# Layer 0 of a four-layer convolution mixer: two channels' banded matrices in one 64x64 block instead of one channel's in a 32x32 block, and tile 0 normalised from two tiles of the input

## The chip, the cores and the metric

The kernel runs on one core of a Trainium2 chip. TensorE (PE) multiplies matrices, VectorE (DVE), ScalarE (ACT) and GpSimd (POOL) work on tiles in on-chip memory, SyncE (SP) and ACT issue most of the transfers. The metric is the device time of one execution in microseconds; the median of the runs before the change is 3408.86 us (3407.19 to 3410.58). All data is float32.

## The reference

The input `x` is (8, 384, 32, 32): 8 images, 384 channels. Four layers follow each other, each behind a group normalisation over 12 neighbouring channels. What matters here is layer 0, which begins with three depthwise 3x3 convolutions of the same normalised input:

```python
def _dwproj(x, dw, g, b, pw):
    y = lax.conv_general_dilated(x, dw, (1, 1), ((1, 1), (1, 1)), feature_group_count=C, ...)
    y = jax.nn.gelu(_bn(y, g, b), approximate=False)      # batch norm over images and pixels
    return jnp.einsum('oc,bchw->bohw', pw, y)
q, k, v = (_dwproj(x, dw, g, b, pw) for each of q, k, v)
attn = softmax(q.T k * scale);  out = bn(w_out @ (attn v))
```

Layer 1 is a mixture of four expert networks, layer 2 a depthwise 7x7 convolution, layer 3 a mixture of small MLPs and depthwise convolutions. They are changed only in the place where a helper and a constant are defined.

## The kernel before

The 384 channels lie in three tiles `ct` of 128 partitions. Layer 0 goes in these stages.

**Statistics.** For each of the 8 images two loads bring tile 0 (into `x0`, L258) and tiles 1 and 2 (into `x`, L259). DVE takes `bn_stats` and `bn_aggr` of each tile and image (L144, L263): 24 pairs (tile, image). `gn_coefs` (L146, L264) then makes scale and shift of the group normalisation for all tiles at once: small matmuls over neighbouring tiles for the mean, four DVE operations, the same matmuls for the variance, a power on GpSimd (L139, `gn_s`), one more DVE operation (`gn_t`).

**Preparing a tile.** `prepare0(ct, b)` normalises an image of a tile on ACT (`affine`, L204) and transposes it in 32x32 blocks on DVE into `xt0s[ct]` (L284), so that the image column lies on the partitions: partition 32 i + (column), and the channel is a free index. For tiles 1 and 2 it first loads the image again into `xn` (3 buffers).

**Convolution.** A 3x3 convolution of one channel is then, for each of three rows of taps, a matmul with a banded 32x32 matrix over the columns. There are 36 groups `n` = (tile, which of q/k/v, u of 4), each with 8 x 4 = 32 channels. In a group (L322 to L333) the host's matrices `w` (384 KB, loaded by ACT's queue three groups ahead, 4 buffers) are used as 32x32 blocks: 2 x 3 x 4 x 4 = 96 matmuls of 32x32 against 256 columns, sixteen positions of the array in turn. The profile records two passes for each float32 matmul, so a group is 192 records. The result fills `ps`, four banks of PSUM; there are two such buffers, all of PSUM. ACT copies `ps` into `o` (L354, 128x2048). Four groups fill one `o` (m = n // 4 counts them, 9 in all); there are two buffers of `o`.

**Results.** While the groups of m run, DVE takes the eight images of m - 1 from `o` (`results`, L299): a transpose back into `y` (4 buffers), two `bn_stats`, and SP writes `y` to `raw` in device memory. After the last m the eight images are taken on their own, the batch norm's coefficients follow (`coefs0`, L210 to L214), and attention begins, which needs them and `raw`.

**Order.** In layer 0 the instructions of PE, ACT and DVE stand in the order in which the program names them (`manual_schedule`); those of GpSimd and SP are placed by a scheduler. In the loop over groups a step names, in this order: the matmuls of `n`, the load of the weights of `n + 3`, the preparations (tile 1 in the four groups of m = 0, two images each; tile 2 in m = 3 to 5), the results of m - 1, and ACT's copy of `n`. Each engine works through its queue in order, so that a waiting instruction holds all behind it.

The changed helper `Banks` (L1113) hands out parts of one PSUM buffer to small matmuls in later layers, and `parity` (L1033 to L1036) is a 128x2 constant: column 0 is one on the partitions of even blocks of 32, column 1 on those of odd blocks. Layer 2 uses it to spread two channels' banded matrices into 64x64 blocks (`next_weights`, L1068, both halves on ACT) and multiplies 64x64 by 64x256 (L1332).

Of the kernel before, what the change touches and what calls it, by code (L numbers as in the profile page):

```python
# [38 lines left out]

# [3 lines left out]
ORDER_0 = ORDER_A.reshape(NC, 4, 4, 8).swapaxes(1, 2).ravel()  # L43
# [30 lines left out]

@with_exitstack
def conv_mixer_kernel(ctx: ExitStack, tc: tile.TileContext, a: dict, out: bass.AP):
# [12 lines left out]
    nc.gpsimd.memset(mhalf, -0.5)  # L89

# [152 lines left out]
    with (  # L243
# [9 lines left out]
        with tc.tile_pool(name="cx", bufs=4) as cx, tc.tile_pool(  # L253
            name="cgn", bufs=2, space=PSUM
        ) as cgn:
            for b in range(B):
                x = cx.tile([P, NC - 1, N], FP, tag="x", name="x")
                nc.sync.dma_start(out=x0[:, b], in_=a["x"][b, :, 0])  # L258
                nc.sync.dma_start(out=x, in_=a["x"][b, :, 1:])  # L259
                for ct in range(NC):  # L260
                    bs = xst[:, ct, 2 * b : 2 * b + 2, :]
                    bn_stats_of(bs, x[:, ct - 1, :] if ct else x0[:, b])
                    nc.vector.bn_aggr(mvx[:, :, ct, b], bs.rearrange("p a s -> p (a s)"))  # L263
            s0, t0 = gn_coefs((mvx[:, 0], mvx[:, 1]), cgn)  # L264

        with tc.tile_pool(name="cy", bufs=3, reuse_waits="tile") as cy, tc.tile_pool(
# [4 lines left out]
            def prepare0(ct, b):  # L271

                if b == 0:
                    pool = cxb if ct == 1 else cxa
                    xt0s[ct] = pool.tile([P, 32, B, H + 2], FP, tag="xt0", name="xt0")
                    for row in (0, H + 1):
                        nc.gpsimd.memset(xt0s[ct][:, :, :, row : row + 1], 0.0)
                if ct == 0:
                    xn = x0[:, b]
                else:  # L280
                    xn = cy.tile([P, N], FP, tag="xn", name="xn")
                    nc.sync.dma_start(out=xn, in_=a["x"][b, :, ct, :])
                affine(xn, xn, s0[:, ct, b : b + 1], t0[:, ct, b : b + 1])
                nc.vector.transpose(  # L284
                    xt0s[ct][:, :, b, 1 : 1 + H].rearrange("p c h -> p h c"), img(xn)
                )
# [4 lines left out]
            def weights_of(n):  # L291
                if n < len(groups):
                    w = cy.tile([P, 2, 4, 3, W], FP, tag="w", name="w", bufs=4)
                    nc.scalar.dma_start(out=w, in_=a["w0"][groups[n]])
                    weights0[n] = w

# [16 lines left out]
            for n in range(3):  # L313
                weights_of(n)
            for b in range(B):
                prepare0(0, b)
            last_o, last = None, None
            for n, (ct, v, u) in enumerate(groups):
# [3 lines left out]
                w = weights0.pop(n)  # L322
                ps = cps.tile([P, 4, 2, B, H], FP, tag="ps", name="ps")
                for cc in range(2):
                    for k in range(3):
                        for j in range(4):
                            for i in range(4):
                                r = slice(32 * i, 32 * i + 32)
                                nc.tensor.matmul(  # L329
                                    ps[32 * j : 32 * j + 32, i, cc],  # L330
                                    lhsT=w[r, cc, j, k, :],
                                    rhs=xt0s[ct][r, 8 * j + 2 * u + cc, :, k : k + H],
                                    start=k == 0, stop=k == 2,  # L333
                                )
                weights_of(n + 3)
                m = n // 4
                if m == 0:
                    for b in (2 * u, 2 * u + 1):
                        prepare0(1, b)
# [693 lines left out]
    parity = lw.tile([P, 2], FP, name="parity", bufs=1)  # L1033
    nc.gpsimd.memset(parity, 0.0)
    for i in range(4):
        nc.gpsimd.memset(parity[32 * i : 32 * i + 32, i % 2 : i % 2 + 1], 1.0)  # L1036
# [76 lines left out]
    class Banks:  # L1113
        def __init__(self):
            self.banks, self.used = tp.tile([P, 4, HF], FP, tag="ps", name="ps"), 0

        def tile(self, shape, *_, **__):
            n = int(np.prod(shape[1:]))
            v = self.banks[: shape[0], self.used, :n]
            self.used += 1  # L1120
            if len(shape) == 3:
                v = v.rearrange("p (a b) -> p a b", b=shape[2])
            if len(shape) == 4:
                v = v.rearrange("p (a b c) -> p a b c", b=shape[2], c=shape[3])
            return v
# [194 lines left out]
    with tc.manual_schedule(engines=ORDERED | {mybir.EngineType.Pool}):  # L1320

        for ct in range(NC):
            o = None
            for c in range(8):
# [28 lines left out]
                if ct == 2 and c == 5:  # L1353
                    norm01 = gn_steps((mv3[:, 0, :2], mv3[:, 1, :2]), Banks, order="B")
                    next(norm01)
# [36 lines left out]
        norm3 = gn_steps((mv3[:, 0], mv3[:, 1]), Banks, order="B")  # L1392
# [8 lines left out]
        pb = Banks().tile([MR, B])  # L1401
# [80 lines left out]
        def hidden3(i):  # L1482


            slot, units = Banks(), []
# [37 lines left out]
        def branch_mean():  # L1523

            hs = atile("hs", [B], MR)
            nc.vector.tensor_add(hs, hsum[:, :, 0], hsum[:, :, 1])
            slot = Banks()
            pa = slot.tile([P, 2, B])
            for j in range(2):
                nc.tensor.matmul(  # L1530
                    pa[:, j], lhsT=mw2[:, j * P : (j + 1) * P], rhs=hs, start=True, stop=True
                )
            nc.vector.tensor_add(mean[:, 1:3], mean[:, 1:3], pa)
            for ct in range(NC):
                nc.vector.tensor_scalar(
                    mean[:, ct], mean[:, ct], 1.0 / N, bsum[:, ct : ct + 1], ALU.mult, ALU.add
                )

            pf = slot.tile([96, B])
            for ct in range(NC):  # L1540
                nc.tensor.matmul(
                    pf, lhsT=fw1[:, ct, :], rhs=mean[:, ct], start=ct == 0, stop=ct == NC - 1
                )
            nc.scalar.activation(g1, pf, AF.Gelu, bias=fb1)
# [3 lines left out]
        def branch_weights():  # L1548

            pg = Banks().tile([P, NC, 3, B])  # L1550
# [60 lines left out]
        def output_bias():  # L1611
            po = Banks().tile([P, NC, B])
# [60 lines left out]
        def first():  # L1673
            wms[0] = weights3(0, Banks())
            c0s[0] = begin(0, 0, pre, 2, nc.gpsimd)
# [64 lines left out]
def lay_out(inp):  # L1740
# [12 lines left out]
    def tiles_0(v):  # L1753
        return tiles(v, ORDER_0)

# [14 lines left out]
    band = band.reshape(3, NC, 4, 4, 4, 2, 3, W, W)  # L1770
    o["w0"] = band.transpose(1, 0, 4, 2, 7, 5, 3, 6, 8).reshape(NC, 3, 4, P, 2, 4, 3, W)
    gb = [np.stack([tiles_0(f[f"L0_conv_{k}_{v}"]) for k in "gb"], 2) for v in qkv]
    o["bn_gb"] = np.concatenate(gb, 1)
    o["bn_gbo"] = np.stack([tiles(f[f"L0_conv_{k}_out"]) for k in "gb"], 2)
    for v in "qk":
        pad = np.zeros((C, NP, 2, 64), np.float32)
        pad[..., 1 : 1 + HD] = f[f"L0_conv_pw_{v}"].T.reshape(C, NP, 2, HD)
        o[f"pw_{v}s"] = tiles_0(pad.reshape(C, NP, P))
        w = f[f"L0_conv_pw_{v}"].T.reshape(C, NP, 3, 32)
        w = np.stack([w[:, :NC, 0], w[:, :NC, 1], w[:, NC], w[:, :NC, 2]], 2)  # L1780
        o[f"pw_{v}"] = tiles_0(w.reshape(C, NC, P))
    o["pw_v"] = tiles_0(f["L0_conv_pw_v"].T)
# [100 lines left out]
```

## Time and profile before

| what | value |
|---|---|
| median of three runs | 3408.86 us |
| the profiled execution | 3404.2 us, its span 3402.5 us |
| statistics end, first normalisation begins | 40.1 us, 50.5 us |
| first and last copy of `ps` begin | 71.8 us, 314.4 us |
| first result's transpose begins | 94.0 us |
| last `bn_stats` of the results ends | 337.8 us |
| PE, 6912 records of L329 | 169.2 us busy |
| DVE, busy from 94 to 338 us | 194.5 us |

Times are from the start of the span. A row of a table of groups reads: line, engine, operation, out<-in, shapes, count | busy time, mean ns of one | idle time before it and what ended it. A row of windows gives the busy time of each engine in a stretch with the number of instructions, the granted TensorE clock as a share of full speed, the busy share of the 16 DMA engines and GB/s.

### The profile page before, as it was taken

How to read it: one execution, taken by the hardware profiler on the slowest of the kernel's cores; microseconds unless marked ns; L12 is line 12 of the kernel's file. 1: busy time of each engine (PE TensorE's matmuls, PEld its weight loads, DVE VectorE, ACT ScalarE, POOL GpSimd, SP SyncE). 2: the span in 40 equal slices, each digit the busy share in tenths (PEclk: the TensorE clock that was granted, in tenths of full speed). 3: DMA queues.
4: the chain of work that ended last, by engine and by line, in shares of the span. 5: the costliest groups of instructions: out<-in, count | busy, mean ns of one | idle time of the engine just before them, and what ended most of it. 6: DMA issues, size and time to landing. Idle time of an engine off the chain costs nothing. (4 is left out here: it accounts for less than half of the span.)

```text
span 3402.5 us, 46860 instructions
## 1 busy us (share of the span) xinstructions
PE 3116.7 (92%) x20224; PEld 1427.8 (42%) x20224; DVE 1608.2 (47%) x2193; ACT 1305.0 (38%) x1339; POOL 157.6 (5%) x361
## 2 busy tenths in 40 slices
PE   3666999999999999999997999999999999985989
PEld 2444334343434333333433444444444444665534
DVE  6787344444454544444453365344333332256164
ACT  3655353544444443535333402122122111556530
POOL 1000000000000000000000000000000000111300
PEclk9988999999999999999998999999999999997999
DMA  6665301011101111110006423121221110676766
GB/s 228 241 245 215 122 21 68 30 58 40 58 22 56 42 56 42 40 56 21 21 22 230 138 64 87 55 76 37 63 72 40 51 42 19 220 243 205 242 202 200
DMA packets 96734, 339.47 MB, mean 100 GB/s; under 512 B 14312, under 2 KB 16960, under 8 KB 91144
## 3 DMA queue, kind: packets, MB, share of 16 engines
q1 hardware_dynamic: 72520, 266.95, 23.2%
q10 hardware_dynamic: 13776, 36.90, 3.5%
q0 software_dynamic: 10224, 32.56, 2.8%
q8 instruction: 160, 2.62, 0.3%
q14 instruction: 54, 0.44, 0.0%
HBM read 237.18 MB, written 102.32 MB: 100 GB/s over the span
## 5 line engine op out<-in xcount | busy, mean ns | idle before, releaser
L552 ACT ACTIVATE e<-sc 128x1024 f32<-128x1024 f32 x512 | 484.3, 1030 | 583.9 <-PE sc L545 583.6
L976 PE MATMUL y<-hs,w 128*128 128x512 f32 x1152 | 521.5, 594 | 6.8 <-DVE hs L961 6.7
L763 PE MATMUL ph<-xn,w 128*128 128x512 f32 x1152 | 525.1, 594 | 0.3 <-ACT xn L204 0.3
L545 PE MATMUL sc<-qT,kT 64*128 64x512 f32 x2048 | 481.0, 606 | 22.6 <-DVE qT L471 15.4
L564 PE MATMUL av<-e,vT 128*64 128x512 f32 x2048 | 469.2, 600 | 0.0
L767 ACT ACTIVATE hs<-ph,b 128x512 f32<-128x512 f32 x192 | 131.6, 685 | 637.9 <-PE ph L763 636.2
L976 PEld LDWEIGHTS y<-hs,w 128*128 128x128 f32 x1152 | 217.2, 190 | 282.6 <-issue 258.6
L763 PEld LDWEIGHTS ph<-xn,w 128*128 128x128 f32 x1152 | 216.4, 190 | 268.2 <-issue 259.4
L545 PEld LDWEIGHTS sc<-qT,kT 64*128 64x128 f32 x2048 | 186.3, 186 | 309.6 <-issue 231.7
L961 DVE TENSOR_TENSOR hs<-hs,cb 128x512 f32<-128x512 f32 x192 | 130.0, 687 | 377.2 <-ACT hs L767 371.3
L564 PEld LDWEIGHTS av<-e,vT 128*64 128x64 f32 x2048 | 136.0, 137 | 319.1 <-issue 319.1
L453 PE MATMUL sc<-y,pw 128*128 128x512 f32 x576 | 252.7, 600 | 11.9 <-DVE kT L471 7.1
L329 PE MATMUL ps<-xt,w 32*32 32x256 f32 x6912 | 169.2, 438 | 99.4 <-issue 99.3
L580 DVE RECIPROCAL inv<-sm 128x512 f32<-128x512 f32 x64 | 214.6, 3353 | 2.2
L578 DVE LOAD_MASK_SELECT sm<-av x64 | 0.9, 14 | 417.1 <-PE av L564 417.1
L329 PEld LDWEIGHTS ps<-xt,w 32*32 32x32 f32 x6912 | 115.2, 110 | 153.1 <-issue 129.5
L1332 PE MATMUL ps<-xt,wx 64*64 64x256 f32 x2688 | 160.8, 399 | 20.1 <-ACT wx L1068 14.7
L453 PEld LDWEIGHTS sc<-y,pw 128*128 128x128 f32 x576 | 109.9, 192 | 154.3 <-issue 146.1
L354 ACT COPY o<-ps 128x2048 f32<-128x2048 f32 x36 | 134.6, 3738 | 101.2 <-PE ps L329 100.5
L966 DVE SCALAR_TENSOR_TENSOR r<-cb,b,r 128x512 f32<-128x512 f32 x192 | 134.3, 745 | 69.1 <-DMA cb<-cfmem 67.5
L1068 ACT ACTIVATE wx<-w,parity 128x448 f32<-128x448 f32 (+2 forms) x192 | 108.3, 616 | 103.3 <-PE ps L1332 32.5
L1332 PEld LDWEIGHTS ps<-xt,wx 64*64 64x64 f32 x2688 | 109.2, 140 | 70.5 <-ACT wx L1068 17.0
(292 smaller groups left out, 2771.5 us busy)
## 6 DMA issues: line engine op xcount, KB each, us to landing
raw<-y SPq DMA_DIRECT2D x72, 512.0 KB
y<-raw SPq DMA_DIRECT2D x24, 1536.0 KB
xr<-in_x SPq DMA_DIRECT2D x42, 512.0 KB
cb<-cfmem SPq DMA_DIRECT2D x64, 256.0 KB
w<-in_w ACTq DMA_DIRECT2D x36, 384.0 KB
x<-in_x SPq DMA_DIRECT2D x16, 768.0 KB
z<-z POOLq DMA_DIRECT2D x16, 768.0 KB, 4.2
r<-z SPq DMA_DIRECT2D x24, 512.0 KB
```

Of the source, the lines that this page charges most:

```text
L329: nc.tensor.matmul(ps[32 * j : 32 * j + 32, i, cc], lhsT=w[r, cc, j, k, :], rhs=xt0s[ct][r, 8 * j + 2 * u + cc, :, k : k + H], start=k == ...
L354: nc.scalar.copy(o.rearrange("p b h (i c) -> p i c (b h)", i=4)[:, :, 2 * u : 2 * u + 2], ps.rearrange("p i c b h -> p i c (b h)"),)
L453: nc.tensor.matmul(ps[:, h, :], lhsT=w[:, ct, pair, :], rhs=y[:, ct, h * HF : (h + 1) * HF], start=ct == 0, stop=ct == NC - 1,)
L545: nc.tensor.matmul(sc[:, s, :], lhsT=kTs[b][r, pair, m * P : (m + 1) * P], rhs=qTs[b][r, pair, h * HF : (h + 1) * HF], start=True, stop=True,)
L552: nc.scalar.activation(e, sc, AF.Exp, scale=1.0 if shifted else HD**-0.5)
L564: nc.tensor.matmul(av[64 * s : 64 * s + 64, :], lhsT=vT[:, m, c0 : c0 + 64], rhs=e[:, s, :], start=m == 0, stop=m == N // P - 1,)
L580: nc.vector.reciprocal(inv, sm)
L763: nc.tensor.matmul(ph, lhsT=w1[:, e, ct, dc * P : (dc + 1) * P], rhs=xn[:, ct, :], start=ct == 0, stop=ct == NC - 1,)
L767: nc.scalar.activation(hs, ph, AF.Relu, bias=b1[:, e, dc : dc + 1])
L966: nc.vector.scalar_tensor_tensor(out=out[oc], in0=cb[e], scalar=b2[:, oc, e : e + 1], in1=out[oc], op0=ALU.mult, op1=ALU.add,)
L976: nc.tensor.matmul(py[oc], lhsT=w2[:, e, dc, oc * P : (oc + 1) * P], rhs=hs, start=k == 0, stop=k == len(TODO) - 1,)
L1332: nc.tensor.matmul(ps[64 * d : 64 * d + 64, 2 * i + e, c % 2], lhsT=w[r, d * K7 + k, :], rhs=xts[ct][r, 16 * d + 8 * e + c, :, k : k + H], ...
```

## The change

The host lays the banded matrices so that two channels are stacked in 64 partitions; `w` has the same bytes. For each group, `spread0` writes them into a `wx` of twice the size: ACT writes the left half (times `parity` column 0), GpSimd the right half (times column 1), so that each 64x64 block holds two channels' 32x32 matrices on its diagonal and zeros beside. A group is then 2 x 3 x 8 = 48 matmuls of 64x64 against 256 columns (96 records). The weights have 3 buffers instead of 4, `wx` has 3; at step `n` the spread of `n + 2` and then the load of `n + 3` are named.

At the start only tiles 0 and 1 are loaded and measured (8 images each), and tile 0 is normalised with coefficients made from them: its groups reach no further than tile 1. The eight images of tile 2 are loaded into `xn` and measured at steps 0 and 1, the mean's matmuls stand on PE after group 1 and the variance's after group 2, each in one of the two PSUM buffers, and the preparation of tile 1 moves from steps 0 to 3 to steps 3, 4, 8, 9 and 10.

```diff
+    parity = const.tile([P, 2], FP, name="parity")
+    nc.gpsimd.memset(parity, 0.0)
+    for i in range(4):
+        nc.gpsimd.memset(parity[32 * i : 32 * i + 32, i % 2 : i % 2 + 1], 1.0)
...
+        def x_stats(ct, b, x):
+            bs = xst[:, ct, 2 * b : 2 * b + 2, :]
+            bn_stats_of(bs, x)
+            nc.vector.bn_aggr(mvx[:, :, ct, b], bs.rearrange("p a s -> p (a s)"))
-        with tc.tile_pool(name="cx", bufs=4) as cx, tc.tile_pool(
+        with tc.tile_pool(name="cx", bufs=8) as cx, tc.tile_pool(
...
-                x = cx.tile([P, NC - 1, N], FP, tag="x", name="x")
+                x = cx.tile([P, N], FP, tag="x", name="x")
                 nc.sync.dma_start(out=x0[:, b], in_=a["x"][b, :, 0])
-                nc.sync.dma_start(out=x, in_=a["x"][b, :, 1:])
-                for ct in range(NC):
...
-            s0, t0 = gn_coefs((mvx[:, 0], mvx[:, 1]), cgn)
+                nc.sync.dma_start(out=x, in_=a["x"][b, :, 1])
+                x_stats(0, b, x0[:, b])
+                x_stats(1, b, x)
+            norms = {0: gn_coefs((mvx[:, 0, :2], mvx[:, 1, :2]), cgn)}
...
-                    w = cy.tile([P, 2, 4, 3, W], FP, tag="w", name="w", bufs=4)
+                    w = cy.tile([P, 24, W], FP, tag="w", name="w")
                     nc.scalar.dma_start(out=w, in_=a["w0"][groups[n]])
...
+            def spread0(n):
+                if n < len(groups):
+                    w = weights0[n]
+                    x = weights0[n] = cy.tile([P, 24, 2, W], FP, tag="wx", name="wx")
+                    nc.scalar.activation(x[:, :, 0, :], w, AF.Copy, scale=parity[:, 0:1])
+                    nc.gpsimd.tensor_scalar(x[:, :, 1, :], w, parity[:, 1:2], None, ALU.mult)
+            def slot0():
+                ps = cps.tile([P, 4, 2, B, H], FP, tag="ps", name="ps")
+                return Slot(ps.rearrange("p i c b h -> p i (c b h)"))
+            def stats2(b):
+                xn = cy.tile([P, N], FP, tag="xn", name="xn")
+                nc.sync.dma_start(out=xn, in_=a["x"][b, :, 2, :])
+                x_stats(2, b, xn)
...
-                        for j in range(4):
-                            for i in range(4):
-                                r = slice(32 * i, 32 * i + 32)
-                                nc.tensor.matmul(
-                                    ps[32 * j : 32 * j + 32, i, cc],
-                                    lhsT=w[r, cc, j, k, :],
-                                    rhs=xt0s[ct][r, 8 * j + 2 * u + cc, :, k : k + H],
+                        for e, d, i in product(range(2), repeat=3):
+                            r = slice(64 * i, 64 * i + 64)
+                            nc.tensor.matmul(
+                                ps[64 * d : 64 * d + 64, 2 * i + e, cc],
+                                lhsT=w[r, 12 * cc + 6 * e + 3 * d + k, :],
+                                rhs=xt0s[ct][r, 16 * d + 8 * e + 2 * u + cc, :, k : k + H],
...
+                spread0(n + 2)
                 weights_of(n + 3)
                 m = n // 4
-                if m == 0:
-                    for b in (2 * u, 2 * u + 1):
-                        prepare0(1, b)
+                if n < 2:
+                    for b in range(4 * n, 4 * n + 4):
+                        stats2(b)
+                if n == 1:
+                    norm = gn_steps((mvx[:, 0], mvx[:, 1]), slot0)
+                    next(norm)
+                if n == 2:
+                    norms[1] = norms[2] = next(norm)
+                for b in {3: (0, 1), 4: (2, 3), 8: (4, 5), 9: (6,), 10: (7,)}.get(n, ()):
+                    prepare0(1, b)
```

`Slot` is the old `Banks` with its PSUM buffer given from outside; later layers call it through a function `banks()`. `parity` leaves layer 2. The order of channels in the host's vectors of layer 0 follows the new stacking.

## The prediction

> **What bounds the kernel now.** I read the stages first, by windows, then who waits in layer 0, then the instructions' order in time, and last the rows of layer 2, which holds the new matmul's form. Layer 0 takes the first 340 us of 3402.5; nothing behind it changes, so a microsecond won before attention begins is won for the whole.
>
> The windows (busy time of PE, PEld, DVE, ACT, POOL; clock; DMA share; GB/s) show PE as good as idle for 50 us while the input is measured, and then no engine full: PE 65 to 70%, DVE 65 to 94%.
>
> ```profile
> 0.00:25.00 25.00, 8.27 (x28) 6.71 (x28) 18.26 (x40) 5.16 (x15) 7.12 (x25) 1.00 0.93 368
> 100.00:150.00 50.00, 33.50 (x1516) 22.84 (x1505) 35.75 (x44) 31.37 (x11) 1.06 (x2) 0.97 0.59 214
> 150.00:225.00 75.00, 48.43 (x2008) 32.71 (x1977) 70.26 (x79) 46.67 (x17) 0.00 (x0) 0.90 0.74 259
> 225.00:300.00 75.00, 52.30 (x2060) 35.42 (x2044) 48.67 (x66) 38.92 (x11) 0.85 (x1) 0.85 0.64 225
> ```
>
> The waits of 94 to 338 us say whom they wait for: DVE for ACT's copies, ACT (page's groups: 100.5 us) for the matmuls, and the matmuls for "issue", that is for nothing but their own instructions.
>
> ```profile
> DVE y L299 <- ACT o L354: 35.8, 6, 10.1
> ...
> PE ps L329 <- issue: 72.4, 44, 4.5
> ```
>
> In order of time the matmuls come in packets of 128 records, 2.75 us long (21.5 ns a record), with 0.7 to 4.5 us between packets:
>
> ```profile
> 115.22 2.74 PE L329 MATMUL ps<-xt,w 32*32 32x256 f32 x127 [2.18 <-issue]
> 119.05 2.74 PE L329 MATMUL ps<-xt,w 32*32 32x256 f32 x128 [1.09 <-issue]
> 122.50 2.75 PE L329 MATMUL ps<-xt,w 32*32 32x256 f32 x128 [0.71 <-issue]
> ```
>
> From the first copy to the last (71.8 to 314.4 us) 35 groups take 6.93 us each, 36 ns a record. So the count of PE's instructions bounds layer 0, except in 150 to 225 us, where DVE is 94% busy. Behind PE stand these:
>
> ```profile
> L354 ACT COPY o<-ps 128x2048 f32<-128x2048 f32 x36 | 134.6, 3738 | 101.2 <-PE ps L329 100.5 <-ACT xn L204 0.8
> L144 DVE BATCH_NORM_STATS2 stats<-y 128x6 f32<-128x512 f32 x144 | 92.7, 686 | 2.5
> L299 DVE STREAM_TRANSPOSE y<-o 128x1024 f32<-128x1024 f32 x72 | 88.4, 1228 | 36.0 <-ACT o L354 35.8
> L284 DVE STREAM_TRANSPOSE xt<-xn 128x1024 f32<-128x1024 f32 x16 | 29.9, 1929 | 22.4 <-ACT xn L204 22.4
> L204 ACT ACTIVATE xn<-xn,gn_t,gn_s 128x1024 f32<-128x1024 f32 x16 | 19.2, 1239 | 0.7 <-DMA xn<-in_x 0.7
> ```
>
> **The change, part by part.**
>
> *Start.* DVE measures one tile of one image every 1.39 us (starts at 37.22 and 38.61), so 16 instead of 24 save 11.2 us; the transfers set nearly the same end: 8.4 MB of input, 1.2 of weights and 0.5 of constants at 368 GB/s are 27.3 us. I put the end at 30 instead of 40.1 us. The normalisation's coefficients take 10.4 us now (40.1 to 50.5). The last tile's mean loses 6 of 12 records of 0.237 us (-1.4), the variance 6 of 14 (-1.3), GpSimd's power 16 columns instead of 24 (a 128x16 row later is 2.91 us, this one 4.21: -1.3): 6.4 us. The first normalisation begins at 36.5 instead of 50.5; the eight transposes end 15.3 us later as now, at 51.8. ACT's first two spreads stand ahead of it and wait for weights; the loads stand behind one that goes out at 20.6 us now, so they land in time.
>
> *Then the third tile's statistics.* They are moved with their eight loads, past nothing on SP but behind all 16 loads of the start; three have free buffers. On DVE they stand behind the transposes: 8 x 1.39 us, plus some 1.2 us for buffers, end at 64. Groups 0 and 1 run beside that (5.2 us each, 1.9 more for the first at a cold clock, where layer 2's first 56 records after idle time take 5.5 us instead of 3.0: 58.9 and 64.1). Then PE's queue holds the mean (3.2 us, to 67.3), and behind it group 2, which also waits for the copy of group 1 (67.9): to 73.1. Behind that the variance (76.2), the power (80.7), and ACT's two normalisations, which stand ahead of the copy of group 3 (to 87.3); the next two images' normalisations and transposes end at 92.6, and only then does DVE take the first result. It does so at 94.0 now. So of 14 us only 1.4 are left, and four of tile 1's transposes (7.4 us) are still owed. This part alone would gain nothing; it counts for what it leaves DVE.
>
> *Matmuls.* Layer 2 in its undisturbed stretch runs the new form:
>
> ```profile
> 2910.00:2940.00 30.00, 30.00 (x556) 20.79 (x550) 0.00 (x0) 21.25 (x23) 3.76 (x10) 1.00 0.30 85
> ```
>
> 556 records in 30 us are 54 ns each; 96 of them make a group 5.18 us instead of 6.93. From group 4 (82.1 us) PE needs 32 x 5.18 = 166 us, at the granted clock of 0.90 of this stretch 184, at 0.85 195. With the last copy (3.7) and the last eight results (19.8) that ends at 290 or 301 us.
>
> The Trainium skill, page "TensorEngine Tiling (Array Packing)", sections "Available Configurations" and "Theoretical Speedup", speaks against the change: 32x32 gives sixteen independent tiles and 64x64 four, so small blocks should pay up to four times more. By it 192 records on sixteen tiles would take half of 96 on four, 2.6 us a group, and the change would cost 36 x 2.6 = 93 us. The trace does not show that rate: 21.5 ns in a packet and 36 ns over all, so the sum goes by these.
>
> *Spread.* ACT's half, 128x768, is not in the trace: by the 128x1024 row 0.93 us, by layer 2's 128x448 spread (616 ns) 1.06; I take 1.0. ACT's queue then needs 4.7 us a group, 172 us for 32 groups with normalisations and GELUs: beside PE and DVE. GpSimd's half has no row of its kind: by a 128x96 copy (279 to 301 ns) 2.3 us, by a 128x84 addition (423 ns) 3.9, by the power (4206 ns for 24 columns) 135. I take 2.3, since a copy with one input is nearest; it is hidden, as its result is wanted two groups later. Ahead of the second power it costs up to 1 us. The skill's "GPSIMD Engine Reference", section 3.1, has 769 ns for 512 elements in its best case, from which 1.2 us is an estimate; no run here shows it.
>
> *DVE, the next bound.* It is 194.5 us busy from 94 to 338. With four more transposes it has 202 us of work behind 92.6, so it cannot end before 294.5. Idle time comes on top: none is the lower end; 6.3%, the idle share of the window where it is busiest now, makes 13.6 us. PE's 290 to 301 lies so close that I take 10: results end at 304.5 instead of 337.8, **33.3 us less**. The transfers of 94 to 338 (232 GB/s x 244 us = 56.6 MB, and 2.1 for tile 1) then need 277 GB/s, a share of 0.78 at the present ratio; that hides them, but not amply. GpSimd's memsets of `parity` at the start (0.1 us each) hide under the loads.
>
> *Sum.* 3404.2 - 33.3 = 3370.9 us against the profiled execution. The median of the runs is 4.7 above that execution: 3375.6, forecast **3375**. Its own range, by the idle time (0 to 13.6) and 3 us of scatter: 3362 to 3383.
>
> **Rivals.**
> 1. *Transfers become the bound.* For: a share of 0.78, a 0.5 MB write every 2.6 us, weights beside them. Against: at 259 GB/s DVE is 94% busy. If 259 is the most, 58.7 MB take 227 us, results end at 319, 18.6 us are won: 3390.
> 2. *The third tile comes late.* Mean, group 2, variance and tile 1 all stand behind its loads. At 214 GB/s eight loads need 2.45 us each, 19.6 in all instead of 12: all later steps move by 7.5 us, 3383.
> 3. *The weights come late.* They are loaded one group ahead of ACT's need instead of three ahead of PE's. Layer 2's spreads waited 12.3 us in 10 waits for such loads. 33 waits of 1.23 us are 41 us at most, and some of it is in DVE's shadow; three quarters would leave no gain, 3400 to 3410. Against: ACT has 5 us for each.
> 4. *The other side: GpSimd is slow.* 33 spreads of d follow one another from 58.9 us; the last group, copy and results add 28.7. Above d = 7.6 us (9.9 ns an element) the kernel is slower than now; at 9 us it ends 47 us later, 3456. For: the power's 175 ns an element. Against: copy and addition lie at 3 and 5 ns.
>
> **How the numbers follow.** Differences under 0.2% (6.8 us) can't be told from no change here. Forecast 0.60, rivals 1 and 2 0.25 together, rival 3 0.06, rival 4 and what I do not see 0.09. Faster: 0.85, same 0.06, slower 0.09. The range for 8 in 10 runs from the forecast's lower end, less 2 us, to beyond rival 1: 3360 to 3400.
>
> **What would show it.** First normalisation near 36.5 us; groups of 96 records with gaps no longer put down to issue; a new wait of PE for DVE's `mvx` after group 1 and of ACT for `gn_t` near 80 us; first result near 92.6; DVE over 90% busy from there to about 304; spreads of 1.0 us on ACT and 2.3 on GpSimd. Wrong it would be with ACT waiting for `w`, with GpSimd's spreads over 5 us, or with DVE waiting for its `y` buffers' writes.

## The result and the profile after

| | before | changed |
|---|---|---|
| median of the runs | 3408.03 us (3403.78 to 3410.58, four) | 3384.26 us (3381.39 to 3390.1, four) |
| profiled execution, its span | 3404.2, 3402.5 us | 3390.1, 3388.4 us |
| first normalisation begins | 50.5 us | 35.0 us |
| first result's transpose begins | 94.0 us | 92.6 us |
| last copy of `ps` begins | 314.4 us | 285.3 us |
| results end (last `bn_stats`) | 337.8 us | 308.8 us |
| DVE busy, idle between first result and results' end | 194.3, 49.5 us | 201.3, 14.9 us |

The ratio of the times is 0.9934, with a 95% interval of 0.9916 to 0.9951: 22.5 us (16.7 to 28.6) faster. The forecast was 3375 us, 9.3 us too low; its range held the time. The profiled execution of the changed kernel is the slowest of its four, so that its 3390.1 us overstate the kernel.

The stages of the changed kernel by windows (PE, PEld, DVE, ACT, POOL; clock; DMA share; GB/s) answer to the ones shown of before:

```profile
100.00:150.00 50.00, 44.42 (x781) 35.75 (x777) 49.48 (x54) 44.55 (x24) 18.66 (x10) 0.97 0.87 295
150.00:225.00 75.00, 66.10 (x1176) 51.07 (x1172) 74.07 (x87) 58.33 (x29) 24.24 (x11) 0.98 0.82 285
225.00:300.00 75.00, 57.70 (x848) 39.03 (x841) 61.77 (x84) 51.01 (x25) 22.89 (x12) 0.89 0.69 245
...
92.60:308.80 216.20, 181.58 (x2916) 133.89 (x2916) 201.28 (x244) 161.36 (x82) 67.99 (x34) 0.94 0.77 270
```

From 100 to 225 us DVE works without a break (99% of both windows): it is the bound. From 225 us on it is not: 61.8 of 75 us, and 13.2 of its 14.9 idle microseconds lie there. The waits of the changed kernel from 80 to 320 us, row by row as engine, line waited for, total, times, longest:

```profile
DVE y L342 <- ACT o L406: 7.8, 3, 5.4
PE ps L373 <- ACT o L406: 16.1, 9, 4.1
PE ps L373 <- POOL wx L328: 9.6, 1, 9.6
...
ACT wx L327 <- DMA w<-in_w: 4.6, 4, 2.3
```

PE's 72.4 us of "issue" are gone, and DVE's wait for ACT's copies has shrunk from 35.8 to 7.8 us. A wait that the prediction does not have is the third row: PE once stood 9.6 us for a spread of GpSimd. The groups of the two spreads, of the matmuls and of the copies (busy, mean ns of one, idle before them):

```profile
L328 POOL TENSOR_SCALAR wx<-w,parity 128x768 f32<-128x768 f32 x36 | 79.3, 2203 | 132.9 <-DMA w<-in_w 65.2 <-PE ps L373 49.2 <-ACT o L406 13.8
L327 ACT ACTIVATE wx<-w,parity 128x768 f32<-128x768 f32 x36 | 33.4, 927 | 19.0 <-DMA w<-in_w 18.9
L373 PE MATMUL ps<-xt,wx 64*64 64x256 f32 x3456 | 199.8, 389 | 47.1 <-DVE xt L309 19.8 <-ACT o L406 16.6 <-POOL wx L328 9.6
L406 ACT COPY o<-ps 128x2048 f32<-128x2048 f32 x36 | 135.1, 3759 | 55.1 <-PE ps L373 33.1 <-DVE y L342 9.5 <-DMA y<-raw 5.0
```

In order of time, the start and then the place of the new wait (start, duration, engine, line, [idle before, releaser]):

```profile
34.99 2.37 ACT L224 ACTIVATE o<-o,gn_t,gn_s 128x1024 f32<-128x1024 f32 x2 [5.69 <-DVE gn_t L209]
...
65.78 0.83 PE L191 MATMUL ps<-mvx,gmatA 128*128 128x8 f32 x6 [1.92 <-DVE mvx L276]
66.99 7.10 PE L373 MATMUL ps<-xt,wx 64*64 64x256 f32 x96 [0.37 <-DVE gn_m L202]
74.02 1.73 PE L191 MATMUL ps<-gn_d,gmatA 128*128 128x8 f32 x14
...
76.53 4.20 POOL L159 TENSOR_TENSOR gn_s<-ve,mhalf 128x24 f32<-128x24 f32 x1
...
80.98 1.24 ACT L224 ACTIVATE xn<-xn,gn_t,gn_s 128x1024 f32<-128x1024 f32 x1 [2.43 <-DVE gn_t L209]
...
92.56 1.20 DVE L342 STREAM_TRANSPOSE y<-o 128x1024 f32<-128x1024 f32 x1
...
256.96 0.88 POOL L159 TENSOR_TENSOR bn_s<-ve,mhalf 128x3 f32<-128x3 f32 x1 [17.82 <-DVE ve L158]
257.84 6.57 POOL L328 TENSOR_SCALAR wx<-w,parity 128x768 f32<-128x768 f32 x3
260.10 23.68 PE L373 MATMUL ps<-xt,wx 64*64 64x256 f32 x384 [9.60 <-POOL wx L328]
288.99 1.25 DVE L342 STREAM_TRANSPOSE y<-o 128x1024 f32<-128x1024 f32 x1 [5.36 <-ACT o L406]
```

The first seven rows follow the prediction step by step up to 92.56 us. The last four are what it lacks. GpSimd's instructions in layer 0 are placed by a scheduler, and it put the power of a batch norm (`bn_s`, inside `coefs0(0)`) ahead of the spreads of the next groups. The power waits 17.8 us for DVE's `ve`; three spreads run only behind it; PE gets the first of them at 260.1 us, after 9.6 us without work; and at 289 us DVE waits 5.4 us for a copy.

### The profile page after: what moved, and what is told of

Same layout as the page of the kernel before. It is cut to its first block, busy times and chain, and to the rows that moved or that the text cites. A ratio compares the mean times of both kernels' runs of the same rounds, so it can differ in the third digit from the quotient of the medians.

```text
span 3388.4 us, 40142 instructions
## 1 busy us (share of the span) xinstructions
PE 3156.8 (93%) x16784; PEld 1467.1 (43%) x16784; DVE 1609.1 (47%) x2199; ACT 1333.1 (39%) x1375; POOL 238.0 (7%) x398
## 3 DMA queue, kind: packets, MB, share of 16 engines
q1 hardware_dynamic: 73672, 266.95, 23.4%
## 4 chain that ended last, share of the span: by engine, by line
PE 68%; issue 10%; DVE 9%; DMA 7%; ACT 4%; POOL 1%; ACTq 0%; SPq 0%; POOLq 0%; DVEq 0%
PE av L616 14%; PE sc L597 13%; PE ph L815 9%; PE y L1028 9%; PE sc L505 7%; PE sc L550 4%; PE sc L655 4%; DVE stats L164 2%; DVE y L342 2%; PE ps L1369 2%; DMA cb<-cfmem 1%; DMA w<-in_w 1%; PE po L1747 1%; PE po L1750 1%; PE po L1758 1%
## 5 line engine op out<-in xcount | busy, mean ns | idle before, releaser
L373 PE MATMUL ps<-xt,wx 64*64 64x256 f32 x3456 | 199.8, 389 | 47.1 <-DVE xt L309 19.8
L373 PEld LDWEIGHTS ps<-xt,wx 64*64 64x64 f32 x3456 | 153.1, 138 | 92.7 <-issue 44.6
L1369 PE MATMUL ps<-xt,wx 64*64 64x256 f32 x2688 | 161.1, 399 | 21.5 <-ACT wx L1116 16.5
L1369 PEld LDWEIGHTS ps<-xt,wx 64*64 64x64 f32 x2688 | 106.5, 140 | 75.0 <-ACT wx L1116 19.7
```

Source lines behind the costliest of these rows:

```text
L373: nc.tensor.matmul(ps[64 * d : 64 * d + 64, 2 * i + e, cc], lhsT=w[r, 12 * cc + 6 * e + 3 * d + k, :], rhs=xt0s[ct][r, 16 * d + 8 * e + 2 ...
L1369: nc.tensor.matmul(ps[64 * d : 64 * d + 64, 2 * i + e, c % 2], lhsT=w[r, d * K7 + k, :], rhs=xts[ct][r, 16 * d + 8 * e + c, :, k : k + H], ...
```

## The experiments

In every run the two landmarks are the first result's transpose and the end of the results. "DVE idle" is the stretch between them less DVE's busy time in it, by windows. "Saved" is one less the ratio, times the median of before measured beside it; where two versions were not measured beside one another, only their "saved" can be compared. Each landmark is from one profile: those of two profiles of one kernel lie up to 3.4 us (results end) and 5.1 us (first result) apart.

| run | first result | results end | DVE idle | ratio, interval | saved us | behind the results |
|---|---|---|---|---|---|---|
| before | 94.0 | 337.8 | 49.5 | | | 3064.6 |
| before, again | 95.2 | 334.4 | 45.0 | | | 3071.0 |
| changed | 92.6 | 308.8 | 14.9 | 0.9934, 0.9916 to 0.9951 | 22.5 | 3079.6 |
| changed, again | 91.6 | 308.2 | 15.2 | 0.9946, 0.9933 to 0.9959 | 18.4 | 3075.9 |
| spread, old start | 97.6 | 310.1 | 17.8 | 0.9928, 0.9916 to 0.9940 | 24.5 | 3074.9 |
| new start, 32x32 | 90.1 | 332.6 | 41.1 | 0.9995, 0.9984 to 1.0006 | 1.7 | 3073.3 |
| GpSimd in order | 95.0 | 305.5 | 9.4 | 0.9929, 0.9915 to 0.9943 | 24.2 | 3071.9 |
| spread on ACT | 94.8 | 308.1 | 12.4 | 0.9900, 0.9885 to 0.9915 | 34.1 | 3075.1 |
| spread on ACT, again | 89.7 | 305.4 | 14.7 | 0.9915, 0.9901 to 0.9928 | 29.0 | 3064.1 |
| wide weights | 92.8 | 311.2 | | 0.9949, 0.9931 to 0.9967 | 17.4 | 3071.9 |
| old start, GpSimd in order | 97.4 | 304.7 | 12.8 | 0.9908, 0.9891 to 0.9925 | 31.4 | 3068.2 |
| the same again | 97.6 | 305.7 | 13.8 | 0.9920, 0.9905 to 0.9936 | 27.3 | 3080.0 |
| old start, spread on ACT | 98.3 | 306.5 | 14.3 | 0.9925, 0.9912 to 0.9939 | 25.6 | 3070.1 |
| short statistics | 90.1 | 283.4 | | 0.9855, 0.9837 to 0.9874 | 49.4 | 3072.7 |

The theory at the outset (A): the 64x64 blocks took away PE's instruction bound, DVE's 201 us of work took its place, the new start is worth nothing, and the rest of the forecast was lost at GpSimd's queue. The rivals (B) differ from run to run and stand in the expectations.

**The changed kernel again.** No edit.

> The changed kernel once more. In its first profile layer 0 ends 29.0 us earlier than before (the last bn_stats of the results ends at 308.8 instead of 337.8 us), but the span is only 14.1 us shorter; 13 to 15 us go between 1790 us and the end, in layers 1 to 3, whose code is the same. Theory A, those layers differ from execution to execution (their transfers): the end of layer 0 lies again within 2 us of 308.8, and what follows it takes again some other time, so that the median is 22 to 29 us below before. Theory B, the change itself slows the later layers (places in memory, the constant made earlier): what follows the end of layer 0 takes again about 15 us longer than before, and the gain stays at 14 to 16 us.

The results end at 308.2 us, within 0.6 us of the first profile, so the landmark of layer 0 stands; behind it this execution was 3.7 us shorter than the other. The time had neither theory: 18.4 us are saved, for 22 to 29 by A and 14 to 16 by B.

**The spread alone.** The old start beside the new blocks:

```diff
-            norms = {0: gn_coefs((mvx[:, 0, :2], mvx[:, 1, :2]), cgn)}
+            s0, t0 = gn_coefs((mvx[:, 0], mvx[:, 1]), cgn)
+            norms = {ct: (s0, t0) for ct in range(NC)}
...
-                if n < 2:
-                    for b in range(4 * n, 4 * n + 4):
-                        stats2(b)
-                if n == 1:
-                    norm = gn_steps((mvx[:, 0], mvx[:, 1]), slot0)
-                    next(norm)
-                if n == 2:
-                    norms[1] = norms[2] = next(norm)
-                for b in {3: (0, 1), 4: (2, 3), 8: (4, 5), 9: (6,), 10: (7,)}.get(n, ()):
-                    prepare0(1, b)
+                if m == 0:
+                    for b in (2 * u, 2 * u + 1):
+                        prepare0(1, b)
```

> The changed kernel with the old start: all three tiles measured first, tile 1 prepared in steps 0 to 3; spreads and 64x64 matmuls stay. Theory A (the forecast's: the start part is only worth what it leaves DVE): the first normalisation begins at 50.5 instead of 35 us, ACT's queue (two normalisations, spread, copy: 7.1 us a group) sets the first four copies, the first result comes near 98 instead of 92.6, but tile 1 is then wholly prepared (7.4 us of DVE work less); results end at 303 to 309 us, the whole within 5 us of the changed kernel. Theory B (the start's 14 us are kept): results end near 322, the whole 13 to 15 us slower than the changed kernel.

The window from its first result to its results' end:

```profile
97.60:310.10 212.50, 185.88 (x3012) 140.14 (x3012) 194.74 (x239) 159.78 (x79) 69.49 (x35) 0.94 0.76 265
```

The first result comes 5.0 us later than in the changed kernel, and the results end only 1.3 us later than its 308.8: DVE has 6.5 us less to do behind the first result (194.7 instead of 201.3). By the ratios it saves 24.5 us where the changed kernel, measured beside it, saves 18.4. The new start gains nothing; theory A holds, with its 303 to 309 us and its 5 us between the two kernels each missed by 1 us. GpSimd's queue does the same here: its power waits 18.1 us for DVE, and PE 9.3 us for the spread behind it.

**The start alone.** The 32x32 blocks kept, the third tile's statistics and tile 1's preparation moved as in the change (the lines of the last diff turned round, in the kernel before, with `gn_steps` and `Slot`).

> The kernel before with the new start alone: two tiles measured first, the third at steps 0 and 1, tile 1 prepared at steps 3, 4, 8, 9, 10; 32x32 matmuls as before. Theory A: the first normalisation begins near 35 us, the first result at 96 to 100 us, and then PE's groups of 6.9 us set the pace: results end at 328 to 340, the whole 0 to 9 us faster than before. Theory B (the start's 14 us are kept): results end near 324, 13 to 15 us faster.

```profile
90.10:332.60 242.50, 163.45 (x5906) 105.97 (x5905) 201.44 (x244) 139.18 (x53) 6.34 (x6) 0.88 0.69 243
```

The first result comes 3.9 to 5.1 us earlier than in the two profiles of before, the results end 1.8 to 5.3 us earlier, and the time can't be told from that of before (0.9984 to 1.0006). The 15 us that ACT starts earlier come to nothing here too. Theory A has the end and the time, but not the first result, which it put at 96 to 100 us. DVE idles 41.1 us, which it does not with 64x64 blocks: the whole gain belongs to these.

**GpSimd in the program's order.**

```diff
-        tc.manual_schedule(engines=ORDERED),
+        tc.manual_schedule(engines=ORDERED | {mybir.EngineType.Pool}),
```

> The changed kernel with GpSimd's instructions of layer 0 in the order in which the program names them, too. In the changed kernel the scheduler put the power of the first batch norm coefficients ahead of the spreads of groups 32 and 33, so that these wait 17.8 us behind it for DVE, PE stands 9.6 us (250.5 to 260.1 us), and at the end DVE waits 5.4 us for the last copy. Theory A, that costs 5 us: the wait of 9.6 us goes, results end at 303 to 305 us instead of 308.8, and the whole is 4 to 6 us faster than the changed kernel. Theory B, DVE would have been as late without it: the wait goes, the end does not move (within 1.5 us).

Windows, then GpSimd and PE in order of time:

```profile
225.00:300.00 75.00, 59.69 (x875) 44.27 (x867) 67.24 (x92) 51.32 (x25) 22.93 (x12) 0.93 0.73 264
95.00:305.50 210.50, 180.10 (x2919) 140.30 (x2916) 201.15 (x244) 161.87 (x82) 68.09 (x34) 0.96 0.79 277
```

```profile
243.47 2.21 POOL L328 TENSOR_SCALAR wx<-w,parity 128x768 f32<-128x768 f32 x1 [2.53 <-DMA w<-in_w]
256.57 2.21 POOL L328 TENSOR_SCALAR wx<-w,parity 128x768 f32<-128x768 f32 x1 [10.90 <-DMA w<-in_w]
258.89 0.88 POOL L159 TENSOR_TENSOR bn_s<-ve,mhalf 128x3 f32<-128x3 f32 x1
...
255.44 21.44 PE L373 MATMUL ps<-xt,wx 64*64 64x256 f32 x384 [2.67 <-ACT o L406]
```

The power now stands where its operand is ready, and no spread waits behind it: the first of the three that had to wait runs at 243.5 instead of 257.8 us. The second comes only 1.3 us earlier than that, at 256.6 us, held by its own weights. PE's packet begins at 255.4 instead of 260.1 us and has no wait for GpSimd. DVE's idle time falls from 15.2 us in the run beside it to 9.4; as the first result comes 3.4 us later here, the results end 2.7 us earlier. The ratios say 5.8 us less time (0.9929 and 0.9946; the intervals overlap). One profile on each side would not be enough, as the ends scatter by some 3 us. But three profiles with the scheduler's order (both of the changed kernel, and the spread alone) have PE's wait of 9.3 to 9.6 us and end at 308.2 to 310.1 us; three in the program's order (this one, and two further down) have no such wait and end at 304.7 to 305.7 us. The place of the power in GpSimd's queue is thus shown to be a cost in layer 0, of about 3 to 5 us; in the whole time it is likely, but the intervals don't show it.

**Both halves of the spread on ACT.**

```diff
-                    nc.gpsimd.tensor_scalar(x[:, :, 1, :], w, parity[:, 1:2], None, ALU.mult)
+                    nc.scalar.activation(x[:, :, 1, :], w, AF.Copy, scale=parity[:, 1:2])
```

> The changed kernel with both halves of the spread on ACT, none on GpSimd. Theory A (GpSimd's 2.2 us a group are hidden, only its place in the queue ahead of two groups costs): ACT's queue grows by 36 x 0.93 = 33 us to 5.6 us a group, 22.4 us for four, beside DVE's 20 to 25; PE's wait of 9.6 us for the spread goes; results end between 306 and 322 us, the whole 0 to 14 us slower than the changed kernel, never faster by more than 3. Theory B (GpSimd's work holds layer 0 back, by its duration or beside VectorE): results end below 304, the whole 5 us or more faster than the changed kernel, although ACT has more to do.

> Both halves of the spread on ScalarE, the same kernel as in the first such run, with more rounds. There the median said 33 us faster than before (over few executions) while the profile's landmark, the end of the results, was no earlier than the changed kernel's (308.1 against 308.2 to 308.8). Theory A (GpSimd's half costs only its place in GpSimd's queue, some 3 to 5 us, and ScalarE's 36 more writes give about that back): results end at 304 to 310, time 20 to 27 us faster than before. Theory B (GpSimd's writes disturb VectorE or the tiles' memory beyond what the waits show): results end at 294 to 303, time 29 to 37 us faster.

A window and the waits of the second run:

```profile
150.00:225.00 75.00, 66.32 (x1182) 44.50 (x1178) 74.01 (x87) 66.32 (x39) 0.00 (x0) 0.98 0.81 279
```

```profile
PE ps L373 <- ACT o L406: 23.4, 12, 3.4
...
DVE y L342 <- ACT o L406: 5.6, 2, 3.8
```

DVE's transposes of results from 90 to 310 us, in the changed kernel and in this run:

```profile
L342 DVE STREAM_TRANSPOSE y<-o 128x1024 f32<-128x1024 f32 x72 | 88.3, 1226 | 10.2 <-ACT o L406 7.8 <-DMA raw<-y 2.4
L342 DVE STREAM_TRANSPOSE y<-o 128x1024 f32<-128x1024 f32 x72 | 88.5, 1229 | 7.9 <-ACT o L406 5.6 <-DMA raw<-y 2.3
```

ACT takes the other half in its idle time (66.3 of 75 us busy instead of 58.3), and PE waits 23.4 us for its copies instead of 16.1 us for copies and 9.6 for GpSimd. The results end at 308.1 and 305.4 us: up to 3.4 us earlier than the changed kernel's, as theory A had it. The time says more: 34.1 and 29.0 us saved, 6.5 to 15.7 more than the changed kernel, as theory B had it. The two kernels were not measured beside one another, and the intervals 0.9901 to 0.9928 here and 0.9916 to 0.9951 there overlap. B's mechanism is not what happened: beside GpSimd's writes and without them a transpose of a result takes 1226 and 1229 ns, a `bn_stats` 685 and 686, so GpSimd doesn't slow these. The rest of the difference is not in the ends of layer 0, and what it comes from stays open: the first of the two profiles is of the slowest of four executions (3384.99 us against a median of 3375.14), so that it can't place what the median gained. By medians measured beside one another this version is level with the old start with GpSimd in order, below (3375.14 against 3374.72 us, and 3376.05 against 3379.85): these two are the fastest found that do all of the work.

**Wide weights.** The host lays the 64x64 blocks out with their zeros; 768 KB a group are loaded, and nothing is spread:

```diff
-                    w = cy.tile([P, 24, W], FP, tag="w", name="w")
+                    w = cy.tile([P, 24, 2, W], FP, tag="w", name="w")
...
-            for n in range(2):
-                spread0(n)
...
-                spread0(n + 2)
```

> The changed kernel without any spread: the weights come from device memory with their zeros, 768 KB a group instead of 384, so that transfers between the first and the last result grow from 58 MB (270 GB/s x 216 us) to 71 MB; ACT and GpSimd have 33 and 79 us less to do. Theory A (DVE bounds layer 0, transfers are hidden at a share of 0.77): 71 MB at the 357 GB/s of a full share are 199 us, still below DVE's 202; the share goes to 0.9 and more, some waits for weights and for the writes of y appear; results end at 303 to 325 us. Theory B (transfers are already the bound at the 270 to 295 GB/s of the busiest windows): 71 MB take 241 to 263 us, results end at 333 to 356, as late as before the change or later.

```profile
100.00:150.00 50.00, 43.24 (x760) 28.77 (x756) 48.15 (x52) 37.15 (x15) 1.07 (x2) 0.97 0.97 356
150.00:225.00 75.00, 65.51 (x1160) 45.06 (x1152) 74.10 (x86) 47.33 (x17) 0.00 (x0) 0.98 0.94 346
```

```profile
ACT o L395 <- DMA raw<-y: 30.5, 7, 7.2
...
DVE y L334 <- DMA raw<-y: 7.1, 3, 4.4
```

The transfers move 346 to 356 GB/s, and DVE still works 74.1 of 75 us. So the 259 GB/s of before, and the 285 of the changed kernel, were no limit. At a share of 0.97 the writes of results begin to be late: ACT's copies wait 30.5 us for them. The results end 2.4 us later, which is no more than the scatter; theory A's 303 to 325 us hold, B's 333 to 356 don't.

**The old start, with GpSimd in order.** The edits of the spread alone and of GpSimd in the program's order together; two runs of it.

> The spread and the 64x64 matmuls with the old start, and GpSimd's instructions of layer 0 in the program's order. Theory A (DVE's work behind the first result sets the end): first result near 97.6 us, 194.7 us of DVE work and 8 to 10 us idle behind it: results end at 300 to 304 us, the whole 2 to 6 us faster than with GpSimd in order alone, and 25 to 31 us faster than before. Theory B (the new start is worth something once the queue is in order): results end at 305 or later, the whole not faster than with GpSimd in order alone.

> The old start with GpSimd's instructions in program order, the same kernel as in the first such run, beside the variants with ScalarE's spread. Theory A (results end 27 to 33 us earlier than before's and all of it reaches the whole): results end at 304 to 306, time 27 to 34 us faster than before. Theory B (the 33 us of the first comparison were a lucky draw of the later layers): time 20 to 26 us faster.

```profile
97.40:304.70 207.30, 183.81 (x3012) 143.40 (x3012) 194.46 (x239) 160.57 (x80) 69.41 (x35) 0.96 0.77 271
```

The results end at 304.7 and 305.7 us, 5.4 and 4.4 us earlier than with the old start and the scheduler's order. DVE idles 12.8 and 13.8 us, more than the 8 to 10 that theory A had; the first end lies between A's 300 to 304 us and B's 305, the second in the 304 to 306 us of its own theory A. 31.4 and 27.3 us are saved: more than the changed kernel's 22.5 and 18.4, though the intervals overlap in part, and with the simpler start.

**The old start, with both halves on ACT.**

> The old start (all three tiles measured first), and both halves of the spread on ScalarE. Theory A (the start is worth nothing, VectorE's 195 us behind a first result at 97 to 98 us set the end, GpSimd's place is worth 3 to 5 us): first result at 96 to 99, results end at 303 to 309, time 24 to 33 us faster than before. Theory B (the start part helps once GpSimd is out of the way, so this one is slower than the new start with ScalarE's spread): results end at 312 to 318, time 15 to 22 us faster than before.

306.5 us and 25.6 us saved, as theory A had it. Its median, 3379.18 us, is 3.1 us above that of the spread on ACT with the new start, measured beside it (3376.05), and their intervals overlap. With GpSimd's spread it was the other way (3382.55 against 3386.86 us). Between the starts no difference is shown.

**Short statistics.**

```diff
-                bn_stats_of(stats[:, v * NC + ct, 2 * b : 2 * b + 2, :], y)
+                for h in range(2):
+                    nc.vector.bn_stats(stats[:, v * NC + ct, 2 * b + h, :], y[:, h * HF : h * HF + 64])
```

> The changed kernel with the batch norm's statistics of the results taken from 64 of each 512 columns, so that it leaves out seven eighths of that work: 144 instructions of 0.69 us become some 0.2 us, DVE's work behind the first result falls from 201 to some 130 us; transfers, matmuls, copies stay. Theory A (DVE is the bound): PE and ACT come next, PE with 184 us from 82 us on, then a copy and a shorter rest of 12 us; results end at 276 to 292 us, 17 to 33 us earlier than 308.8. Theory B (transfers or PE bound it, DVE is only busy beside them): results end within 8 us of the present, apart from the shorter rest after the last copy (20 to 12 us), so at 293 to 301.

```profile
150.00:225.00 75.00, 70.89 (x1269) 58.01 (x1265) 50.61 (x88) 64.38 (x32) 28.80 (x14) 0.98 0.86 311
```

```profile
DVE y L342 <- ACT o L407: 25.7, 4, 8.9
```

With less to do DVE is 50.6 of 75 us busy, the results end 25.4 us earlier than the changed kernel's, and DVE waits for ACT's copies again. Of the 25.4 us, 17.9 lie ahead of the last copy (it begins at 267.4 instead of 285.3 us); the other 7.5 are the shorter work behind it, which either theory has. Theory B's 293 to 301 us are missed by 10. DVE is shown to be the bound of the changed kernel. How near the next bound lies is shown too: some 25 us on, where PE is 95% busy.

**Before, again.** No edit.

> The kernel before once more, for a second profile of its later part. In its first profile 3064.6 us lie between the end of layer 0's results and the end of the span; in the profiles of the changed kernel and its variants, whose later code is the same, 3068 to 3080. Theory A (the later part of one and the same code varies by some 10 us from execution to execution, and the first profile of before drew a short one): results end at 337.5 to 338.5, behind it 3066 to 3080 us. Theory B (layer 0's end at an earlier time really costs the later layers some 8 us, as something else that starts with the kernel has to be ready): again 3062 to 3066.

Its later part is 3071.0 us, inside theory A's 3066 to 3080. Its results end at 334.4 us, which neither theory had: layer 0 of the kernel before varies by at least 3.4 us from execution to execution.

## Why the prediction was right, and where it was off

*The bound and its successor: right.* PE's instructions bounded layer 0; with half as many of them, 72.4 us of "issue" are gone, and DVE is 99% busy for 125 us. The run with short statistics shows DVE as the bound, the run with the start alone shows that nothing is won without the 64x64 blocks. That it is the number of the matmuls, and not their shape, that made the pauses is argued from the packets of 128 records between them; no run changes the one without the other.

*The start: right to a microsecond or two.* First normalisation 36.5 forecast, 35.0 measured; the third tile's statistics end at 65.7 us for 64, group 2 at 74.1 for 73.1, the power at 80.7 for 80.7, the first result at 92.56 for 92.6. The sentence "this part alone would gain nothing" holds in the run that made it alone. That the sum comes out to a tenth of a microsecond is luck. Errors in it cancel: the mean's last matmuls and what follows before group 2 took 1.2 us (65.78 to 66.99) for 3.2, group 2 took 7.1 us for 5.2. And in the seven profiles with this start and the larger blocks the first result begins at 89.7 to 95.0 us; DVE waited 0.7 us for the last load of the third tile in the earliest, 3.8 us in the latest.

*Durations: right.* ACT's half 0.93 us for 1.0, GpSimd's 2.20 for 2.3: the 128x96 copy was the right row. The page "GPSIMD Engine Reference", section 3.1, of the Trainium skill, from which 1.2 us was an estimate, gives its best case; the 2.20 us measured are 1.8 times that estimate. 384 records in 20.95 to 23.68 us are 55 to 62 ns each, for 54 forecast. The page "TensorEngine Tiling (Array Packing)", section "Theoretical Speedup", which spoke for sixteen small tiles, is not borne out: the run that kept them, with the new start, ends layer 0 at 332.6 us, the one with the larger blocks at 308.8.

*DVE's work: right.* 201.3 us for 202, behind the first result at 92.6.

*DVE's idle time: this term was mis-sized.* "I take 10" measured 14.9, and so 304.5 became 308.8 us (4.9 us more idle, 0.7 less work). I put the idle time down to PE lying close. For what goes beyond the 10 us the runs show something else: "it is hidden, as its result is wanted two groups later" was said of GpSimd's spread by its duration, and the queue that it stands in was priced only at the second power of the start ("up to 1 us"). The scheduler's power of `coefs0(0)` holds the spreads 17.8 us, more than the two groups (10.4 us) that they were ahead. With GpSimd in order the idle time is 9.4 us and the results end at 305.5, which is the forecast within 1 us; with the old start the same step takes it from 17.8 to 12.8 and 13.8 us. So the queue's place makes 4.0 to 5.8 us of idle time, as much as the term was too small. The 10 us themselves are not confirmed as closely as 9.4 looks: without any spread on GpSimd, and so without this wait, DVE idles 12.4 to 14.7 us, PE then waiting longer for ACT. No rival had the queue's case; the fourth had GpSimd's spread as slow, not as badly placed.

*What reaches the whole: less than forecast.* "A microsecond won before attention begins is won for the whole" made 33.3 us. Layer 0 gave 29.0 by the profile of before that the prediction had, and 25.6 by the second one; the whole gave 22.5 and 18.4. The part behind layer 0 has the same code in all versions, and it took 3064.1 and 3075.1 us in two profiles of one kernel, 3068.2 and 3080.0 in two of another. Against such a scatter, one profile on each side can't say whether the missing 3 to 11 us are lost or drawn. About half of it, or more, is PE's own busy time. The shortest and the longest of these later parts, of the second spread on ACT and of the second old start in order, by windows:

```profile
305.40:3369.50 3064.10, 2917.68 (x13220) 1292.38 (x13220) 1350.84 (x1862) 1130.11 (x1256) 139.32 (x324) 0.98 0.26 85
305.70:3385.70 3080.00, 2925.47 (x13220) 1290.68 (x13220) 1351.19 (x1862) 1129.80 (x1256) 137.98 (x324) 0.97 0.26 85
```

For the same 13220 records PE is busy 2917.7 and 2925.5 us, while DVE and ACT differ by less than 0.4 us. Over the thirteen profiles other than that of short statistics PE's busy time behind the results goes from 2915.3 to 2925.5 us. Four of them have a granted clock of 0.97 there, and their later parts take 3074.9 to 3080.0 us; the nine with 0.98 take 3064.1 to 3075.9. So the later part is, by and large, longer where PE was granted less; the changed kernel has 0.97 in one profile and 0.98 in the other, so that no effect of the change on it is shown.

Over the twelve comparisons "saved" differs from the gain in layer 0 (against the mean of before's two ends, 336.1 us) by -9.5 to +6.1 us, -3.1 in the mean, so most of a gain does arrive. That the changed kernel loses more than the others is not excluded.

*The rivals.* Transfers as a bound: no, by the wide weights at 346 GB/s; forecast share 0.78, measured 0.77. Third tile late: by 1.7 us of the 7.5, and by 3.5 in the run with GpSimd in order. Weights late: behind the first result ACT waits 4.6 us in four waits. GpSimd slow: no.

## What to carry to other kernels

Where the matmuls wait for nothing but their own instructions, half as many larger ones pay even though half of each is zeros (here 54 ns a record for 36); then price what the next engine has to do, and expect the end to be set there. Work that is hidden by its duration is not hidden by its place: on a queue that a scheduler fills, look which waiting instruction stands ahead of it. A start that is made earlier is worth what the engine that ends last gains by it, here nothing.

## What the runs showed of the hardware that was not expected

The same code behind layer 0 differs by 4 to 12 us between two profiles of one kernel, up to half of this change's gain, and the longest of these parts go with a granted clock of 0.97 instead of 0.98. DVE was not seen to be slowed by anything beside it: from 150 to 225 us its transposes of results took 1226 ns with GpSimd 24.2 us busy, 1227 with it idle, and 1226 with the transfers at a share of 0.94. The granted clock rose rather than fell with the larger blocks: 0.98 instead of 0.90 from 150 to 225 us, 0.94 on average from the first result to the end of the results.
